# Aggregation of a graph layer with the gathered rows as the stationary side, 40 columns streaming, and a ninth row buffer

## The chip, the core and the metric

The kernel runs on one core of one Trainium2 chip. The metric is the device time of one execution in microseconds (us); lower is better. The median of three runs stands for a kernel. One more execution is recorded by the hardware profiler, and the rows in this document come from such recordings.

## The reference

There are N = 12500 nodes with D = 128 features and M = 200000 edges, sorted by destination node. All is float32. Cut to what matters:

```python
h = relu(layernorm(x))
Qv, Ku = h @ W_Q.T, h @ W_K.T
score = einsum('md,md->m', Qv[dst], Ku[src]) / sqrt(128) * exp(-edge_weight)
keep  = rank of the edge among its node's edges < 16        # the 16 best edges of a node
w     = where(keep, exp(score - max over the node's kept edges), 0)
alpha = w / (sum of w over the node)
agg   = segment_sum(alpha[:, None] * (h[src] @ W_msg.T), dst)
out   = x + relu(h @ W_self.T + agg)
```

The kernel sums the rows first and multiplies by W_msg afterwards: per node it forms the sum over edges of w times h[src], and then divides by the sum of w and multiplies by W_msg.

## The kernel before

**Prologue.** The node rows are normalised and written to a table `h_tab` in HBM. Constants are made, and the gathers of the first groups start.

**Groups and chunks.** The edges are cut into chunks of 128 edges, one edge to a partition, and 14 chunks make a group (`GC` = 14; there are `G` = 112 groups). A group's window of nodes can begin inside its last chunk and end in the first chunk of the next group, so each group works on up to 15 chunks (`NJ` = 15): chunk 14 of a group reads the first row block of the next group. Because the edges are sorted, the edges of chunk j of a group fall on 40 neighbouring nodes (`WN` = 40) that begin at 8·j − 16 in the group's window of 128 nodes.

**Gathers.** For each chunk GpSimd (POOL) issues one indirect DMA that fetches 128 rows of `h_tab`, 512 bytes each, into one block of the tile `hs` (128 partitions x 14 blocks x 128). `let_go(g, k)` does this for two chunks: VectorE (DVE) copies their indices to a small tile `ix`, and POOL issues the gathers. `hs` has 8 buffers, so the first gather of group g must wait until the last reader of group g − 8 is through. Two late blocks of some groups (`lateSP`, `lateACT`) are fetched row by row from the queues of SyncE (SP) and ScalarE (ACT) instead.

**The loop.** The order of the work is written out by hand. Step i of the loop holds stages of several groups: `q_to_edges` and `scores` for group i, `slots_by_node` and `slots_out` for i − 1, `best`, `kept_to_edges`, `on_edges`, `exps` for i − 2, `weights`, `sums` and `sums_out` for i − 3, the turning and `products` for i − 4, `output` and `store` for i − 5; `far_of`, `edges_turned`, `away` and `places` prepare the node patterns of group i + 1. Each engine works through its own list in this order. The pieces of the gathers are let go by `more(0)` to `more(6)`, spread over the step: `more(0)` after `weights`, `more(1)` just before `best`, `more(2)` just after it, `more(3)` and `more(4)` among the scores, `more(5)` after the second half of `sums`, `more(6)` at the end. In the steady loop `more(0)` to `more(4)` let go pieces 2 to 6 of group i + 4, and `more(5)` and `more(6)` pieces 0 and 1 of group i + 5.

**The banks.** The tile `et` is one PSUM bank: columns 0 to 151 take `slots_by_node`, 256 to 296 `node_by_slots`, and 384 to 511 the sums. The tile `so` is another: four blocks of 128 columns for the turned rows, the queries, the turned sums, and the products. One more bank, `a`, is passed back and forth by TensorE (PE) and ACT in `far_of`, `edges_turned` and `away`.

**The aggregation.** `weights` (L734) writes, for each chunk, the 128 x 40 pattern of edge weights into `alz`, in which a chunk has a stretch of 160 columns that is zero elsewhere. `sums` (L744) then runs one float32 matmul for each chunk: the stationary side is a slice of 128 columns of `alz`, mostly zeros, placed so that the 40 filled columns lie at the chunk's nodes; the streaming side are the 128 gathered rows' 128 features. All 15 add up to one 128 x 128 block, nodes by features. Half of them (`sums(g, 0)`, seven chunks) stand in the middle of a step, the other half (`sums(g, 1)`, eight chunks) after the third block of queries. A float32 matmul shows as two weight loads (LDWEIGHTS, engine PEld) and two matmuls (PE) in the trace. `sums_out` (L749) copies the block out of PSUM and scales each node by the reciprocal `rden`; `sums_turned` (L752) turns it on PE, `sums_turned_out` (L756) copies it out, and `products` (L759, L760) multiplies by the two weight matrices and adds.

Of the kernel before, what the change touches and what calls it, by code (L numbers as in the profile page):

```python
# [10 lines left out]
F32 = mybir.dt.float32  # L11
# [4 lines left out]
AF = mybir.ActivationFunctionType  # L16
# [9 lines left out]
P = 128  # L26
# [9 lines left out]
GC = 14  # L36
NJ = GC + 1

KM = 40

WN = 40
# [14 lines left out]
PRE = 16  # L56
STEP = 8
WW = STEP * (NJ - 1) + WN
# [3 lines left out]
def lead(j):  # L62
    return STEP * j - PRE
# [7 lines left out]
def upper(ap):  # L71

    return ap.bitcast(BF16).rearrange("p (n two) -> p n two", two=2)[:, :, 1]
# [8 lines left out]
def gnn_layer(  # L82
# [27 lines left out]
    nc = tc.nc  # L110
    N, D = x.shape
# [18 lines left out]
    const = ctx.enter_context(tc.tile_pool(name="const", bufs=1))  # L130
# [7 lines left out]
    def bank(tag, bufs):  # L138
        return psum.tile([P, 512], F32, tag=tag, bufs=bufs, name=tag)

    ident = const.tile([P, P], F32, name="ident")
    ones = const.tile([P, 1], F32, name="ones")
    onerow = const.tile([1, P], F32, name="onerow")
    zrow = const.tile([1, WW], BF16, name="zrow")


    alz = [const.tile([P, NJ * (WW + STEP)], F32, name=f"alz{i}") for i in range(2)]
    sl1 = [const.tile([P, NJ, KM + 1], F32, name=f"sl1{i}") for i in range(2)]
    slots = const.tile([P, KM], F32, name="slots")
    nvec = const.tile([P, 1], F32, name="nvec")  # L150
# [5 lines left out]
    wmsgT = const.tile([P, P], F32, name="wmsgT")  # L156
# [16 lines left out]
    rows_pool = ctx.enter_context(tc.tile_pool(name="rows", bufs=1))  # L173
# [3 lines left out]
    T = [{} for _ in range(G)]  # L177

    def gather(g, j0, j1, index, table=h_tab):
        if j0 == 0:  # L180
            T[g]["hs"] = rows_pool.tile([P, GC, D], F32, name="hs", bufs=8)
        for j in range(j0, j1):
            nc.gpsimd.indirect_dma_start(  # L183
                out=T[g]["hs"][:, j, :], out_offset=None, in_=table[0:N, :],
                in_offset=bass.IndirectOffsetOnAxis(ap=index(j), axis=0))
# [7 lines left out]
    for name, (_, _, p0, rate, j) in STREAMS.items():  # L193
        m = 0
        while rate:
            ready = p0 + (P * m + P - 1) // rate + 1
            g = max(ready, RAW)
# [62 lines left out]
    def raw_begun(g):  # L260
        normed(T[g]["hs"], 0, 1, *T[g]["raw"])
# [28 lines left out]
    with tc.tile_pool(name="edges", bufs=1) as ep, ExitStack() as stage:  # L290
# [51 lines left out]
        nc.gpsimd.iota(nvec, pattern=[[0, 1]], base=0, channel_multiplier=1,  # L342
                       allow_small_or_imprecise_dtypes=True)

        jj, eq = (alz[0][0:32, NJ * KM * k:NJ * KM * (k + 1)].rearrange("p (j k) -> p j k", k=KM) for k in range(2))
        nc.gpsimd.iota(jj, pattern=[[1, NJ], [0, KM]], base=0, channel_multiplier=0,
                       allow_small_or_imprecise_dtypes=True)
        nc.gpsimd.iota(dst_r, pattern=[[1, RL + P]], base=1 << 21, channel_multiplier=0)
# [2 lines left out]
        k = RF if REM else RF - 1  # L351
# [2 lines left out]
                              bass.AP(dst.tensor, dst.offset + p0 * RW - HALO, [[RW, p1 - p0], [1, RL + P]]))  # L354
        nc.sync.dma_start(dst_r[k:k + 1, 0:HALO + M - k * RW], dst[k * RW - HALO:M].rearrange("(p c) -> p c", p=1))
        load_rows(ew_r, ew)
        nc.gpsimd.memset(alz[1], 0.0)
        nc.vector.memset(ones, 1.0)
        nc.vector.memset(onerow, 1.0)
        nc.vector.memset(zrow, 0.0)  # L360
# [39 lines left out]

        for j in range(NJ):
            nc.vector.memset(w0[:, j:j + 1], float(lead(j)))
        nc.vector.memset(alz[0], 0.0)
        for k in range(2):
            nc.vector.memset(sl1[k][:, :, KM:], 1.0)
        for g in range(2):
# [43 lines left out]
        for j0 in range(0, NJ, 4):  # L450
            j1 = min(j0 + 4, NJ)
            pt = bank("q", 3)
            for j in range(j0, j1):
                nc.tensor.matmul(pt[:, (j - j0) * RR:(j - j0 + 1) * RR], lhsT=rel[:, j * P:(j + 1) * P],
                                 rhs=upper(ident[0:RR, 0:RR]), start=True, stop=True)
# [87 lines left out]
    with tc.tile_pool(name="win", bufs=2) as win:  # L543

        so = bank("s", 1)
        et = bank("e", 1)

        def rows_of(g, j):
            if (g, j) in slow:
                return T[g]["late", j]  # L550
            return T[g]["hs"][:, j, :] if j < GC else T[g + 1]["hs"][:, 0, :]
# [179 lines left out]
        def weights(g):  # L731
            n, kept = chunks[g], T[g]["kept"]
            nc.vector.tensor_tensor(kept[:, 0:n], T[g]["up"][:, 0:n], kept[:, 0:n], op=OP.mult)
            nc.vector.tensor_tensor(alz[g % 2].rearrange("e (j w) -> e j w", w=WW + STEP)[:, 0:n, 0:WN],  # L734
                                    T[g]["ow"][:, 0:n, :], bc(kept[:, 0:n], WN), op=OP.mult)


        def sums(g, part, at=None):
            n = chunks[g]
            if part == 0:  # L740
                T[g]["pa"] = et[:, 384:384 + P] if at is None else at
            half = n // 2
            for j in range(half) if part == 0 else range(half, n):
                nc.tensor.matmul(T[g]["pa"], lhsT=alz[g % 2][:, WW * j + PRE:WW * j + PRE + P],  # L744
                                 rhs=rows_of(g, j), start=(j == 0), stop=(j == n - 1))

        def sums_out(g):
            T[g]["agn"] = win.tile([P, D], F32, name="agn")
            nc.scalar.activation(T[g]["agn"], T[g]["pa"], AF.Copy, scale=T[g]["rden"])  # L749

        def sums_turned(g):
            nc.tensor.transpose(so[:, 2 * P:3 * P], T[g]["agn"], ident)  # L752

        def sums_turned_out(g):
            T[g]["aggT"] = win.tile([P, P], F32, name="aggT")
            nc.scalar.copy(T[g]["aggT"], so[:, 2 * P:3 * P])  # L756

        def products(g):
            nc.tensor.matmul(so[:, 3 * P:4 * P], lhsT=T[g]["hT"], rhs=wselfT, start=True, stop=False)  # L759
            nc.tensor.matmul(so[:, 3 * P:4 * P], lhsT=T[g]["aggT"], rhs=wmsgT, start=False, stop=True)  # L760

        def output(g):
            T[g]["o"] = win.tile([P, D], F32, name="o")
# [50 lines left out]
        def at(g, stage, *args):  # L814
            if 0 <= g < G:
                stage(g, *args)


        for i in range(-3, G - 1):
            at(i + 3, load_nodes)  # L820
            for k, _ in enumerate(rows_named("SP", i)):
                rows_asked("SP")
                if k == 0:
                    at(i - 1, load_x)
            if not rows_at.get(("SP", i)):
                at(i - 1, load_x)
            if i == G - 2:
                load_x(G - 2)
                load_x(G - 1)
            if i == 8:  # L830
                nc.sync.dma_start(h_tab[N:N + P, :], zpad)
                nc.sync.dma_start(x_end[XT:XT + P, :], zpad)
                nc.sync.dma_start(x_end[0:XT, :], x[N - XT:N, :])
            def raw(part):
                if i in (1, 2):
                    raw_finished(i + 1, part)

            def more(k):

                if i in (-1, 0, 1):  # L840
                    g = i + 6
                else:
                    g, k = (i + 4, k + 2) if k < 5 else (i + 5, k - 5)
                    if g < 8:
                        return
                if i >= -1 and g < G:
                    let_go(g, k)

            at(i, q_to_edges, 0)
            at(i - 5, output)  # L850
            at(i - 5, store)
            at(i - 3, weights)
            more(0)
            at(i - 4, sums_turned)
            at(i + 1, far_of, 0)
            at(i - 4, sums_turned_out)
            at(i + 1, q_out)
            at(i, q_to_edges, 1)
            at(i + 1, far_of, 1)
            rows_asked("ACT", ACT_ROWS // 8)  # L860
            raw(0)
            for b in range(3):
                at(i - 1, slots_by_node, b)
            at(i + 1, far_of, 2)
            more(1)
            at(i - 2, best)
            more(2)
            at(i - 2, sum_of_exps)
            at(i - 1, slots_out)
            raw(1)  # L870
            at(i, q_to_edges, 2)
            at(i + 1, far_of, 3)
            raw(2)
            at(i + 2, h_turned)
            at(i, scores, 0)
            more(3)
            at(i + 1, to_edges)
            rows_asked("ACT", ACT_ROWS * 5 // 16)
            at(i + 2, h_turned_out)
            at(i - 2, kept_to_edges)  # L880
            at(i - 1, node_by_slots)
            at(i + 1, edges_turned)
            at(i - 3, sums, 0)
            at(i, scores, 1)
            more(4)
            at(i + 1, away, 0)
            at(i, q_to_edges, 3)
            at(i - 2, one_over_sum)
            at(i + 1, away, 1)
            rows_asked("ACT")  # L890
            at(i - 3, sums, 1)
            at(i, scores, 2)
            at(i - 2, on_edges)
            more(5)
            at(i + 1, away, 2)
            at(i - 3, sums_out)
            at(i - 4, products)
            at(i - 2, exps)
            at(i + 1, places)
            for _ in rows_named("ACT", i + 1):  # L900
                pass
            rows_asked("ACT", ACT_ROWS * 3 // 8)
            at(i, scores, 3)
            at(i, scores_in_slots)
            if i == 0:
                raw_stats(2)
                raw_stats(3)
                raw_begun(2)
                raw_begun(3)
            if i in (1, 2):  # L910
                raw_finished(i + 1, 3)
            more(6)
            at(i + 2, q_made)
            if i > 0 and later:
                later.pop(0)()
# [3 lines left out]
        blocks = -(-chunks[L] // 4)  # L919

        def turned(g):
            sums_turned(g)
            sums_turned_out(g)

        def begun(g):
            sums(g, 0, bank("a", 1)[:, 0:P])

        def all_slots(g):
            for b in range(3):
# [78 lines left out]
    with tc.tile_pool(name="gen", bufs=1) as gen, tc.If(nc.values_load(  # L1008
# [116 lines left out]
        with tc.For_i(0, NT, 1) as T:  # L1125
# [16 lines left out]
            _, e16, rden = softmax_rest(gen, cand[:, 0:TOPK])  # L1142
# [40 lines left out]
```

## Time and profile before

| what | value |
|---|---|
| median of three runs | 3100.45 us (3090.87 to 3109.37) |
| the profiled execution, its own time | 3112.28 us |
| its span from the first to the last instruction | 3110.5 us |
| mean granted TensorE clock over the span | 0.741 of full speed |
| busy: PE, PEld, DVE, ACT, POOL | 66%, 54%, 41%, 33%, 47% of the span |
| DMA | 144.38 MB, mean 46 GB/s |

In the rows, the columns of a group are: line, engine, operation, out<-in, shapes and count, then busy time in us and the mean in ns of one, then the idle time of the engine just before them with what ended it. In a timeline they are start, duration, engine, line, operation, count, and in brackets the idle time before it with its releaser. The releaser "remote" means that the semaphore moved when no recorded instruction of this core ended. PE rows end where a model puts the end of the matmul, so neighbouring matmuls overlap in them; the distance from start to start is the throughput.

### The profile page before, as it was taken

The page shows a single profiled execution, that of the slowest core. Times are in us where ns is not written, and L with a number is a line of the kernel's source. Part 1 is how long each engine was busy: PE and PEld are TensorE (multiplying, and loading weights), DVE is VectorE, ACT ScalarE, POOL GpSimd, SP SyncE. Part 2 cuts the span into 40 slices and gives each one's busy share as a digit, 9 for nine tenths or more (in the row PEclk, how much of TensorE's full clock was granted, in tenths as well). Part 3 has the DMA queues.
Part 4 walks back from the last instruction along what each step waited for, and adds up shares of the span by engine and source line. Part 5 has one row for each costly group of instructions (what it writes and reads, how often), then busy time and mean ns, then how long its engine had stood idle before and what let it go on. Part 6 is the DMA issues. An engine that isn't in the chain of part 4 may idle for free. (4 is left out here: it accounts for less than half of the span.)

```text
span 3110.5 us, 55712 instructions
## 1 busy us (share of the span) xinstructions
PE 2052.1 (66%) x13800; PEld 1692.2 (54%) x13801; DVE 1264.1 (41%) x7016; ACT 1041.8 (33%) x2190; POOL 1457.7 (47%) x1529
## 2 busy tenths in 40 slices
PE   0256666666677667676676666776676666667667
PEld 0145555555555555555565555555565555555556
DVE  4453334433344334443433333434434433344346
ACT  4443323333333233333333333333333332333333
POOL 6524444444444444444444445444445444444440
PEclk9867777767777776777777777767767777777779
DMA  8201111111111111111111111111111111111110
GB/s 218 62 24 43 50 43 42 43 39 44 43 42 44 42 44 42 43 42 42 44 44 42 42 43 44 42 40 43 44 44 44 43 42 42 44 43 41 42 40 12
DMA packets 113004, 144.38 MB, mean 46 GB/s; under 512 B 36775, under 2 KB 86567, under 8 KB 111904
## 3 DMA queue, kind: packets, MB, share of 16 engines
q0 software_dynamic: 48512, 99.39, 12.6%
q1 hardware_dynamic: 59038, 40.04, 4.7%
q8 instruction: 109, 1.79, 0.2%
q14 instruction: 225, 1.84, 0.2%
q10 hardware_dynamic: 5120, 1.32, 0.2%
HBM read 126.79 MB, written 14.40 MB: 45 GB/s over the span
## 5 line engine op out<-in xcount | busy, mean ns | idle before, releaser
L183 POOL DMA_INDIRECT hs<-h_tab,ix x1456 | 1394.9, 958 | 1540.6 <-PE e L744 605.4
L744 PEld LDWEIGHTS e<-hs,alz 128*128 128x128 f32 x3142 | 612.1, 296 | 291.9 <-issue 280.5
L744 PE MATMUL e<-hs,alz 128*128 128x128 f32 x3142 | 668.9, 393 | 0.0
L642 PE MATMUL q<-q,to_e 128*128 128x128 f32 x3348 | 589.9, 324 | 44.9 <-issue 42.9
L642 PEld LDWEIGHTS q<-q,to_e 128*128 128x128 f32 x3348 | 545.9, 234 | 121.5 <-issue 87.5
L604 ACT ACTIVATE far<-a,minus 128x512 bf16<-128x512 f32 (+1 forms) x447 | 294.6, 659 | 891.9 <-issue 344.2
L653 DVE SCALAR_TENSOR_TENSOR prod<-hs,dec_all,q 128x128 f32<-128x128 f32 x1623 | 470.2, 342 | 133.6 <-remote 60.1
L602 PE MATMUL a<-rel,ident 112*128 112x512 bf16 (+1 forms) x447 | 211.0, 472 | 426.0 <-issue 264.4
L627 ACT ACTIVATE aw<-a 128x400 bf16<-128x400 f32 x336 | 169.4, 504 | 836.7 <-PE a L625 450.4
L683 DVE TENSOR_SCALAR ell<-slots,e 128x40 f32<-128x40 f32 x112 | 27.9, 249 | 933.6 <-remote 390.2
L625 PE MATMUL a<-minus_at,pdT 32*128 32x400 bf16 x336 | 146.6, 436 | 376.1 <-ACT aw L627 245.4
L669 PE MATMUL e<-opo,sl 128*41 128x40 f32 x3348 | 236.9, 252 | 34.0 <-issue 33.9
L669 PEld LDWEIGHTS e<-opo,sl 128*41 128x41 f32 x3348 | 215.7, 168 | 43.5 <-issue 31.3
L667 PEld LDWEIGHTS <-zrow 1*41 1x41 bf16 x112 | 11.3, 101 | 412.3 <-issue 412.2
L609 ACT ACTIVATE to_e<-far 128x1920 f32<-128x1920 bf16 x112 | 201.3, 1797 | 3.4
L764 DVE SCALAR_TENSOR_TENSOR o<-s,x_t 128x128 f32<-128x128 f32 x112 | 32.6, 291 | 403.2 <-ACT up L729 350.1
L625 PEld LDWEIGHTS <-pdT 32*128 32x128 bf16 x336 | 31.4, 94 | 190.5 <-ACT pdT L618 122.9
L631 ACT ACTIVATE opo<-aw 128x1200 f32<-128x1200 bf16 x112 | 134.7, 1202 | 0.1
L653 DVE DVE_READ_ACCUMULATOR prod<-hs,dec_all,q 128x1 f32 x1623 | 132.0, 81 | 0.0
L219 DVE COPY ix<-idx_all 128x2 int32<-128x2 int32 (+1 forms) x747 | 126.1, 183 | 0.0
L712 PEld LDWEIGHTS <-to_e 128*128 128x128 bf16 x1674 | 68.0, 111 | 94.4 <-DVE km L695 88.0
L712 PE MATMUL x<-km,to_e 128*128 128x43 bf16 x1674 | 76.7, 202 | 58.4 <-DVE km L695 58.3
(197 smaller groups left out, 1868.0 us busy)
## 6 DMA issues: line engine op xcount, KB each, us to landing
lateSP<-h_tab SPq DMA_DIRECT2D x3968, 0.5 KB
lateACT<-h_tab ACTq DMA_DIRECT2D x2560, 0.5 KB
hs<-h_tab,ix POOLq DMA_INDIRECT x1456
h_r<-h_tab SPq DMA_DIRECT2D x112, 64.0 KB
x_t<-in_x_dram SPq DMA_DIRECT2D x108, 64.0 KB
out_dram<-o SPq DMA_DIRECT2D x108, 64.0 KB
xg<-in_x_dram SPq DMA_DIRECT2D x2, 1400.0 KB
h_tab<-xg SPq DMA_DIRECT2D x2, 1400.0 KB
```

What stands on the lines that cost most here:

```text
L183: nc.gpsimd.indirect_dma_start(out=T[g]["hs"][:, j, :], out_offset=None, in_=table[0:N, :], in_offset=bass.IndirectOffsetOnAxis(ap=index(j ...
L602: nc.tensor.matmul(pr[:, 0:n1 - n0], lhsT=upper(ident[0:RR, g:g + 1]).to_broadcast([RR, P]), rhs=rel[:, n0:n1], start=True, stop=True)
L604: nc.scalar.activation(T[g]["far"][:, n0:n1], pr[:, 0:n1 - n0], AF.Square, bias=minus)
L609: nc.scalar.activation(T[g]["to_e"][:, 0:n], T[g]["far"][:, 0:n], AF.Relu, bias=1.0, scale=-1.0)
L625: nc.tensor.matmul(pr[:, 0:400], lhsT=T[g]["pdT"], rhs=minus_at.rearrange("k w j s -> k (w j s)")[:, n0:n1], start=True, stop=True)
L627: nc.scalar.activation(T[g]["aw"][:, n0:n1], pr[:, 0:400], AF.Square)
L631: nc.scalar.activation(T[g]["opo"].rearrange("e w j s -> e (w j s)"), T[g]["aw"], AF.Relu, bias=1.0, scale=-1.0)
L642: nc.tensor.matmul(pq[:, (j - j0) * P:(j - j0 + 1) * P], lhsT=T[g]["to_e"][:, j * P:(j + 1) * P], rhs=T[g]["q"], start=True, stop=True)
L653: nc.vector.scalar_tensor_tensor(prod, rows_of(g, j), dec_all[:, c:c + 1], T[g]["pq", b][:, (j % 4) * P:(j % 4 + 1) * P], op0=OP.mult, op1 ...
L669: nc.tensor.matmul(et[0:KM + 1, STEP * j:STEP * j + WN], lhsT=sl1[g % 2][:, j, :], rhs=T[g]["ow"][:, j, :], start=False, stop=(j == n - 1))
L712: nc.tensor.matmul(px[:, j, 0:KM + 3], lhsT=upper(T[g]["to_e"][:, j * P:(j + 1) * P]), rhs=upper(T[g]["km"]), start=True, stop=True)
L744: nc.tensor.matmul(T[g]["pa"], lhsT=alz[g % 2][:, WW * j + PRE:WW * j + PRE + P], rhs=rows_of(g, j), start=(j == 0), stop=(j == n - 1))
```

## The change

- The aggregation is turned round. The stationary side is now a chunk's gathered rows (128 edges x 128 features), the streaming side the chunk's 40 columns of weights, and the result has features on the partitions and nodes along the columns. Each chunk adds to its own 40 columns of a stretch of 152, so one more matmul with a row of zeros first opens the whole stretch.
- `alz` shrinks from 15 x 160 to 15 x 40 columns; its two memsets go, and the helper tiles that lay in it in the prologue get tiles of their own.
- The result is already turned. `sums_out` becomes a plain copy; `messages` multiplies it by W_msg (a float32 matmul where the transpose was); `messages_out` scales by `rden` while it copies out; `products` adds that with an identity matmul.
- `hs` has nine buffers, and in the loop every piece of the gathers belongs to one group later than before: pieces 2 to 6 of group i + 5 and pieces 0 and 1 of group i + 6. Step 2 lets go a whole group (8).

```diff
-    alz = [const.tile([P, NJ * (WW + STEP)], F32, name=f"alz{i}") for i in range(2)]
+    alz = [const.tile([P, NJ, WN], F32, name=f"alz{i}") for i in range(2)]
...
-            T[g]["hs"] = rows_pool.tile([P, GC, D], F32, name="hs", bufs=8)
+            T[g]["hs"] = rows_pool.tile([P, GC, D], F32, name="hs", bufs=9)
...
-        jj, eq = (alz[0][0:32, NJ * KM * k:NJ * KM * (k + 1)].rearrange("p (j k) -> p j k", k=KM) for k in range(2))
+        jj, eq = (ep.tile([32, NJ, KM], F32, name=f"jk{k}") for k in range(2))
...
-        nc.gpsimd.memset(alz[1], 0.0)
...
-        nc.vector.memset(alz[0], 0.0)
...
-            nc.vector.tensor_tensor(alz[g % 2].rearrange("e (j w) -> e j w", w=WW + STEP)[:, 0:n, 0:WN],
+            nc.vector.tensor_tensor(alz[g % 2][:, 0:n, :],
                                     T[g]["ow"][:, 0:n, :], bc(kept[:, 0:n], WN), op=OP.mult)
...
             if part == 0:
-                T[g]["pa"] = et[:, 384:384 + P] if at is None else at
+                T[g]["pa"] = et[:, 304:304 + WW] if at is None else at
+                nc.tensor.matmul(T[g]["pa"], lhsT=zrow[:, 0:P], rhs=zrow, start=True, stop=False)
             half = n // 2
             for j in range(half) if part == 0 else range(half, n):
-                nc.tensor.matmul(T[g]["pa"], lhsT=alz[g % 2][:, WW * j + PRE:WW * j + PRE + P],
-                                 rhs=rows_of(g, j), start=(j == 0), stop=(j == n - 1))
+                nc.tensor.matmul(T[g]["pa"][:, STEP * j:STEP * j + WN], lhsT=rows_of(g, j),
+                                 rhs=alz[g % 2][:, j, :], start=False, stop=(j == n - 1))
 
         def sums_out(g):
+            T[g]["aggT"] = win.tile([P, P], F32, name="aggT")
+            nc.scalar.copy(T[g]["aggT"], T[g]["pa"][:, PRE:PRE + P])
+
+        def messages(g):
+            nc.tensor.matmul(so[:, 2 * P:3 * P], lhsT=T[g]["aggT"], rhs=wmsgT, start=True, stop=True)
+
+        def messages_out(g):
             T[g]["agn"] = win.tile([P, D], F32, name="agn")
-            nc.scalar.activation(T[g]["agn"], T[g]["pa"], AF.Copy, scale=T[g]["rden"])
-
-        def sums_turned(g):
-            nc.tensor.transpose(so[:, 2 * P:3 * P], T[g]["agn"], ident)
-
-        def sums_turned_out(g):
-            T[g]["aggT"] = win.tile([P, P], F32, name="aggT")
-            nc.scalar.copy(T[g]["aggT"], so[:, 2 * P:3 * P])
+            nc.scalar.activation(T[g]["agn"], so[:, 2 * P:3 * P], AF.Copy, scale=T[g]["rden"])
 
         def products(g):
             nc.tensor.matmul(so[:, 3 * P:4 * P], lhsT=T[g]["hT"], rhs=wselfT, start=True, stop=False)
-            nc.tensor.matmul(so[:, 3 * P:4 * P], lhsT=T[g]["aggT"], rhs=wmsgT, start=False, stop=True)
+            nc.tensor.matmul(so[:, 3 * P:4 * P], lhsT=ident, rhs=T[g]["agn"], start=False, stop=True)
...
             def more(k):
-                if i in (-1, 0, 1):
+                if i in (-1, 0, 1, 2):
                     g = i + 6
                 else:
-                    g, k = (i + 4, k + 2) if k < 5 else (i + 5, k - 5)
-                    if g < 8:
+                    g, k = (i + 5, k + 2) if k < 5 else (i + 6, k - 5)
+                    if g < 9:
                         return
...
-            at(i - 4, sums_turned)
+            at(i - 4, messages)
...
-            at(i - 4, sums_turned_out)
+            at(i - 4, messages_out)
```

The calls after the loop, for the last groups, change in the same way.

More of the change, by code (lines that the diff above doesn't have):

```diff
@@ L921, in turned @@
         def turned(g):
-            sums_turned(g)
-            sums_turned_out(g)
+            messages(g)
+            messages_out(g)
         def begun(g):
-            sums(g, 0, bank("a", 1)[:, 0:P])
+            sums(g, 0, bank("a", 1)[:, 0:WW])
         def all_slots(g):
```

## Prediction

> **What bounds the kernel now.** I read the page first: no engine is full.
>
> ```profile
> span 3110.5 us, 55712 instructions
> ...
> PE 2052.1 (66%) x13800; PEld 1692.2 (54%) x13801; DVE 1264.1 (41%) x7016; ACT 1041.8 (33%) x2190; POOL 1457.7 (47%) x1529
> ```
>
> POOL, which issues the gathers, idles for half of the span, so I asked its waits next (total us, times, longest).
>
> ```profile
> POOL hs L183 <- PE e L744: 605.4, 99, 7.9
> POOL hs L183 <- DVE prod L653: 462.0, 106, 6.2
> ```
>
> There are about 106 laps of one group each, and in nearly each the first gather waits for `sums`. The timeline shows the lap: eight gathers, a pause, six gathers, a pause.
>
> ```profile
> 1504.56 0.95 POOL L183 DMA_INDIRECT hs<-h_tab,ix  x1 [7.72 <-PE e L744]
> ...
> 1513.60 0.94 POOL L183 DMA_INDIRECT hs<-h_tab,ix  x1 [0.30 <-issue]
> 1518.66 0.94 POOL L183 DMA_INDIRECT hs<-h_tab,ix  x1 [4.11 <-DVE prod L653]
> ...
> 1524.90 0.94 POOL L183 DMA_INDIRECT hs<-h_tab,ix  x1 [0.30 <-issue]
> 1531.98 0.95 POOL L183 DMA_INDIRECT hs<-h_tab,ix  x1 [6.13 <-PE e L744]
> ```
>
> What happens in the pauses, from the timeline of all engines, is one chain:
>
> ```profile
> 1511.83 0.38 PE L602 MATMUL a<-rel,ident 112*128 112x512 bf16 x1 [3.53 <-ACT far L604]
> 1512.30 2.32 PE L669 MATMUL e<-opo,sl 128*41 128x40 f32 x30
> 1516.26 0.25 DVE L683 TENSOR_SCALAR ell<-slots,e 128x40 f32<-128x40 f32 x1 [8.64 <-PE a L602]
> 1518.23 0.16 DVE L219 COPY ix<-idx_all 128x2 int32<-128x2 int32 x1
> 1524.34 0.17 DVE L719 TENSOR_TENSOR up<-up,s 128x15 f32<-128x15 f32 x1 [2.08 <-remote]
> 1527.38 0.50 ACT L627 ACTIVATE aw<-a 128x400 bf16<-128x400 f32 x1 [5.68 <-remote]
> 1528.36 3.78 PE L744 MATMUL e<-hs,alz 128*128 128x128 f32 x16
> ```
>
> One lap is 1531.98 − 1504.56 = 27.42 us: 9.04 to the eighth gather; 2.66 until `ell` starts, although the PE work that it reads (L669) ended at 1514.62, 1.64 before; 2.40 until the next gather; 6.24 to the sixth; 2.48 until ACT's `aw`; 0.98 until the second half of `sums`; 3.62 from there to the next lap's first gather. In the two pauses nothing runs that would account for the first 1.6 us, and the waits there are put down to "remote" or to work long done. Such waits belong to the gathers: L719 follows L718 on the same engine, 2.08 us late here, 0.03 us late in a stretch without gathers.
>
> ```profile
> 228.37 0.20 DVE L718 TENSOR_REDUCE up<-x 128x15 f32<-128x45 f32 x1
> 228.60 0.17 DVE L719 TENSOR_TENSOR up<-up,s 128x15 f32<-128x15 f32 x1
> ```
>
> So I read: while gathers are in flight, hand-overs between instructions are late, and what waits is let go some 1.6 us after the last gather of a batch. PE, ACT and DVE work that ends before that costs nothing. Of all that the change touches, only the 3.62 us of the second half of `sums` lie on the path.
>
> **The change part by part.**
>
> *Sums, second half (16 load-and-matmul pairs).* How long is a pair whose load is 128 columns and whose stream is 40? No such pair is in the trace. The parts are, at the same low clock: the first load of a run alone, with 128 and with 41 columns, and a matmul within a run, with 128 and with 40.
>
> ```profile
> L744 PEld LDWEIGHTS e<-hs,alz 128*128 128x128 f32 x1 | 0.3, 287 | 4.6 <-issue 4.6
> L669 PEld LDWEIGHTS e<-opo,sl 128*41 128x41 f32 x1 | 0.1, 145 | 0.1
> L744 PE MATMUL e<-hs,alz 128*128 128x128 f32 x11 | 2.6, 421 | 0.0
> L669 PE MATMUL e<-opo,sl 128*41 128x40 f32 x26 | 2.0, 269 | 0.0
> ```
>
> Loads: (287 − 145)/(128 − 41) = 1.63 ns a column, so 128 columns are 209 ns. Streams: (421 − 269)/88 = 1.73 ns a row, and eleven L744 matmuls take 2.6 us, of which the pace is (2.6 − 0.42)/10, about 0.21 us (0.2135 from the starts of the 16: (3.78 − 0.16 − 0.42)/15). So a load of 128 costs what a stream of 128 costs, and the two overlap: in turn they would be 0.42. With a 40-row stream the load remains, and the pace stays at 0.2135. I take that: turning the sum round trades a stream for nothing, since the load was the same length all along. Bounds for the pace: 0.0707 from L669, (2.32 − 0.27)/29, if only the stream counted; 0.209 + 0.067 = 0.276 if a short stream could no longer cover the next load. What remains is the shorter last stream: 0.421 − 0.269 = −0.15 us a lap.
>
> *The clock.* The mean over all matmuls of L744 in the loop, and over the last groups:
>
> ```profile
> L744 PE MATMUL e<-hs,alz 128*128 128x128 f32 x3142 | 668.9, 393 | 0.0
> L744 PE MATMUL a<-hs,alz 128*128 128x128 f32 x104 | 13.1, 279 | 0.2 <-DVE alz L734 0.2
> 3080.44 3.59 PE L744 MATMUL a<-hs,alz 128*128 128x128 f32 x30
> ```
>
> One takes 421 ns at the low clock and 279 at the high one, where 30 have a pace of (3.59 − 0.28)/29 = 0.114. The mean 393 says that (393 − 279)/(421 − 279) = 0.80 run at the low clock. The granted clock around a second half, and in the batch behind it:
>
> ```profile
> 1500.93:1504.64 3.71, 3.71 (x17) 3.48 (x17) 1.42 (x8) 0.50 (x1) 0.09 (x1) 0.50 0.01 2
> 1505.40:1508.20 2.80, 2.80 (x24) 2.69 (x24) 1.30 (x5) 1.75 (x4) 2.19 (x3) 0.99 0.27 73
> ```
>
> (Columns: busy us and count of PE, PEld, DVE, ACT, POOL; granted clock; DMA share; GB/s.) 3.7 us of solid matmuls at 0.50 are followed by 0.99. If what counts is the stream, it is solid no longer after the change (about 67 of 213 ns), the clock is not raised, and the 20% at the high clock go too: 14 x 0.20 x (0.2135 − 0.114) = +0.28 us a lap. [...]
>
> Together: (−0.15 + 0.28) x 106 = +13 us. If the clock is raised as before, it is −0.15 x 106 = −16; if it falls, the 22 or so 128x128 matmuls of L759 to L642 behind (2.80 us) lose 22 x 0.0995 = 2.2 us, hidden beneath the eight gathers: PE has 3.53 us of idle before L602 at 1511.83 and `ell` waits 1.64 us beyond L669. I cost that at nothing.
>
> *Sums, first half, and the zero matmul* lie under the six gathers; the zero matmul is like L667's. *The turned copy, `messages`, `products`*: a float32 matmul in two passes for the one-pass transpose, one pair for another in `products`, the same two ACT copies in the other order: about one pair (0.3 us) more, under the eight gathers.
>
> ```profile
> L667 PE MATMUL e<-zrow 1*41 1x152 bf16 x112 | 31.2, 278 | 0.0
> L752 PE MATMUL s<-ident,agn 128*128 128x128 f32 x112 | 30.7, 274 | 3.0 <-DVE rden L705 1.9 <-DVE o L764 1.0
> ```
>
> Cover gone, they would cost 0.28 + 0.27 us a lap, +58; I take 0 in the loop and +1 for the last groups, where nothing is gathered.
>
> *Ninth buffer, one group more ahead.* With eight buffers, the first gather of i + 5 overwrites group i − 3; with nine, that of i + 6 also overwrites i − 3. The same wait stands at the same place, on the same half of `sums`, with the same POOL queue behind it. Rows arrive a lap earlier, and no wait for gathered rows is among POOL's or PE's large ones. At the start one step (2) gains a batch; at the end one more step runs without gathers:
>
> ```profile
> 207.00:225.00 18.00, 11.95 (x71) 9.43 (x71) 9.99 (x50) 9.16 (x20) 0.00 (x0) 0.63 0.05 13
> 3049.00:3067.00 18.00, 16.80 (x164) 14.33 (x163) 10.80 (x58) 10.65 (x23) 0.00 (x0) 0.91 0.03 9
> ```
>
> A step without gathers takes about 18 us, one with them 27, so +9 and −9: 0, bounds −9 and +9.
>
> *The last groups* have no cover and the high clock: at the low one, 104 matmuls x 0.0995 = +10; I take +8.
>
> *Prologue.* Two memsets go, on POOL and DVE, worth −4.3 if both were on the path and 0 if neither; I take −2.
>
> ```profile
> L357 POOL MEMSET alz<- 128x2400 f32 x1 | 2.3, 2282 | 0.0
> L403 DVE MEMSET alz<- 128x2400 f32 x1 | 2.1, 2058 | 0.5 <-issue 0.5
> ```
>
> **Sum:** +13 + 1 + 0 + 8 − 2 = +20 on the profiled execution's own 3112.3, so 3132. It stands 0.4% over the median of the runs; times 3100.45/3112.28 = 0.9962 that is **3120 us**.
>
> **The rivals.**
>
> 1. *The clock is raised as before* (loads count as work): −16 − 1 = −17, 3095, as a median 3083. For it: PEld is as busy as PE in the solid stretch. Against: L669's stretch, loads and streams of equal length, tells nothing apart.
>
> 2. *Load and stream go in turn, each at half the pace I gave it.* The trace allows that reading: 213.5/256 = 0.83 ns a column, load and stream added up, and L669's 70.7/81 = 0.87. Then 128 + 40 columns cost 140 ns. The pace now is 0.80 x 0.2135 + 0.20 x 0.114 = 0.194 in the mean, so 14 x (0.140 − 0.194) − 0.15 = −0.90 a lap, −96; with the last groups (104 x 0.026 = +3) and −1, −94: 3018, as a median 3007. Against: the first load's own length, 287 against 145. [...]
>
> 3. *The load is cheap and overlaps*: half of the slope, 0.1045 us: 14 x (0.1045 − 0.194) − 0.15 = −1.40 a lap, −148, with −2 for the rest 2962, as a median 2951.
>
> 4. *Slower by more: the clock's fall is not covered.* The 2.2 us lost behind the second half pass through to `ell`. Place: PE before L669; it decides as soon as the cover is under 2.2. With the 1.64 of `ell` as cover it is 0.55 x 106 = 58 more, 3190, as a median 3178. For it: the same clock rules the whole batch. Against: 3.53 us of idle on PE before it.
>
> That the change doesn't do what it says can be for the ninth buffer only, and is in the sum as such.
>
> **How the numbers follow.** My forecast (pace kept by the load, clock low) has 0.42; rival 1 0.15; rival 2 0.22, since one slope of modelled ends speaks against it; rival 3 0.08; rival 4 0.13. Measurement can tell about 0.5%, 15.5 us. The forecast is +20 of unknowns of about ±15: slower 0.27, same 0.15. Rival 1, at −17, is split, faster 0.07 and same 0.08. Rivals 2 and 3 are faster, 4 slower. So faster 0.37, same 0.23, slower 0.40. The range from 3005 to 3180 takes in all but rival 3 and what lies beyond rivals 2 and 4. The forecast's own range is 3100 to 3140.
>
> **What would show it right or wrong.** Right: the second half of `sums` as 16 matmuls at 0.21 us from start to start, their durations 0.27, granted clock 0.50 in them and in the eight gathers' first microseconds; 99 or so waits of POOL for L743's matmuls of about 6 us; laps of 27.4. A pace of 0.14 or less is rival 2 or 3; 0.99 after the second half is rival 1; `ell` right behind L669's end is rival 4. The forecast is wrong altogether if POOL's first gather no longer waits for `sums`, or if the batches of gathers change in length.

## The result and the profile after

The changed kernel takes 3176.8 us against 3098.7 us, a ratio of 1.0255 (95% interval 1.022 to 1.0289): +78 us. In the two profiled executions the spans differ by 65.1 us. The page of the changed kernel, its header, busy times and the clock in 40 slices:

```profile
span 3175.6 us, 56157 instructions
...
PE 2284.1 (72%) x14024; PEld 1916.6 (60%) x14025; DVE 1268.7 (40%) x7015; ACT 1045.3 (33%) x2190; POOL 1450.2 (46%) x1528
...
PEclk9966666656666666666656666666666566666666
```

Only PE and PEld are clearly busier; the granted clock has fallen from 0.741 to 0.657 in the mean. The queries of the kernel before, then the queries and the sums of the changed one (count, busy us, mean ns):

```profile
L642 PE MATMUL q<-q,to_e 128*128 128x128 f32 x3348 | 589.9, 324 | 44.9 <-issue 42.9
```

```profile
L640 PE MATMUL q<-q,to_e 128*128 128x128 f32 x3348 | 732.3, 388 | 25.1 <-issue 24.4
...
L743 PE MATMUL e<-alz,hs 128*128 128x40 f32 x3142 | 666.5, 391 | 0.0
L743 PE MATMUL a<-alz,hs 128*128 128x40 f32 x104 | 20.6, 377 | 0.0
```

Turning the sums did next to nothing to their own busy time in the loop (668.9 us before). In the last groups (tile `a`) they take 377 ns apiece instead of 279, and the queries, which the change does not touch, went from 324 to 388. The wait of POOL for the sums stands where it stood (99 times, 605.4 us before):

```profile
POOL hs L183 <- PE e L743: 673.3, 102, 15.4
POOL hs L183 <- DVE prod L651: 466.6, 107, 6.0
```

A second half of the sums, from the timeline:

```profile
1522.03 0.49 PE L623 MATMUL a<-minus_at,pdT 32*128 32x400 bf16 x1 [4.26 <-ACT aw L625]
1522.45 3.64 PE L743 MATMUL e<-alz,hs 128*128 128x40 f32 x16
1525.93 0.94 POOL L183 DMA_INDIRECT hs<-h_tab,ix  x1 [6.09 <-PE e L743]
```

From its start to POOL's next gather it is 3.48 us where the lap quoted in the prediction had 3.62. In the 63 halves of the changed kernel that show as one run of 16, the pace after the first pair is 0.2133 us from start to start, and from the start of the half to the gather it is 3.54 us in the mean, as it was before. So that stretch neither gained nor lost. Where the 65.1 us went, by three marks that both traces have (the pattern L661, now L659, of the sixth group and of the ninth from the end):

| stretch | before | after | difference |
|---|---|---|---|
| start to the sixth group's pattern | 283.7 | 291.9 | +8.2 |
| 98 steps of the loop | 2638.4 | 2677.1 | +38.7 |
| from there to the end | 188.4 | 206.6 | +18.2 |

And one lap, in its parts, as a mean over the laps of each trace:

| part of the lap | before | after |
|---|---|---|
| first to last of the eight gathers | 8.90 | 8.81 |
| to the first of the six | 5.32 | 5.37 |
| first to last of the six | 5.65 | 5.66 |
| to the second half of the sums | 3.71 | 4.12 |
| to the next lap's first gather | 3.33 | 3.37 |
| lap | 26.91 | 27.33 |

The loss sits in the part ahead of the second half, and there it has two values: about 3.5 us in some laps, about 5.1 in others. Before, 20 of 110 laps are over 4.5 us, after the change 44. A lap of the long kind, from the changed kernel's timeline:

```profile
1481.73 0.69 ACT L602 ACTIVATE far<-a,minus 128x512 bf16<-128x512 f32 x1 [4.02 <-remote]
...
1482.84 1.91 PE L640 MATMUL q<-q,to_e 128*128 128x128 f32 x8
...
1484.40 0.95 POOL L183 DMA_INDIRECT hs<-h_tab,ix  x1 [4.46 <-DVE prod L651]
1484.55 0.52 PE L600 MATMUL a<-rel,ident 112*128 112x384 bf16 x1
1485.11 0.58 ACT L602 ACTIVATE far<-a,minus 128x384 bf16<-128x384 f32 x1 [0.90 <-PE a L600]
1485.72 1.80 ACT L607 ACTIVATE to_e<-far 128x1920 f32<-128x1920 bf16 x1
...
1490.67 0.95 POOL L183 DMA_INDIRECT hs<-h_tab,ix  x1 [0.30 <-issue]
1492.98 0.26 ACT L616 CAST pdT<-a 32x128 bf16<-32x128 f32 x1 [4.82 <-remote]
1493.30 0.51 PE L623 MATMUL a<-minus_at,pdT 32*128 32x400 bf16 x1 [3.58 <-ACT pdT L616]
1493.74 1.65 PE L640 MATMUL q<-q,to_e 128*128 128x128 f32 x6
1495.32 0.51 PE L623 MATMUL a<-minus_at,pdT 32*128 32x400 bf16 x1
1495.76 2.35 PE L743 MATMUL e<-alz,hs 128*128 128x40 f32 x10
```

and the same step in the short lap that the prediction walked through, from the timeline of the kernel before:

```profile
1512.24 0.69 ACT L604 ACTIVATE far<-a,minus 128x512 bf16<-128x512 f32 x1
...
1518.97 1.80 ACT L609 ACTIVATE to_e<-far 128x1920 f32<-128x1920 bf16 x1
...
1521.45 0.26 ACT L618 CAST pdT<-a 32x128 bf16<-32x128 f32 x1
...
1522.83 0.94 PE L642 MATMUL q<-q,to_e 128*128 128x128 f32 x6
```

In the short lap the second `far` goes through while gathers still start (the last at 1513.60); `to_e` ends 2.11 us after the first of the six gathers (1518.66), `pdT` is cast at once, and `away` and six queries are done beneath the batch. In the long lap that `far` is held until after the eight gathers (4.02 us, "remote"), all behind it comes later, `to_e` ends 3.12 us after the first of the six, and now the hand-over to `pdT` is held as well, 4.82 us, until 2.3 us after the last gather. `away`, six queries at a granted clock of 0.50 (1.65 us, where the short lap's six take 0.94 at 1.00) and `away` again then stand between the batch and the sums. Over the laps, `to_e` ends mostly either about 2.1 or about 3.1 us after that gather: up to 2.2 us the cast was early in 79 of 79 laps before and 54 of 54 after, over 2.8 us it was late in 22 of 22 and 38 of 39. Between the two lie 2 laps before and 9 after.

At the end of the program the clock is lower too (columns as in the prediction), first of the kernel before, then of the changed one:

```profile
3080.00:3095.00 15.00, 11.30 (x124) 10.35 (x125) 13.20 (x65) 2.54 (x11) 0.30 (x1) 1.00 0.02 7
3095.00:3110.50 15.50, 7.19 (x65) 6.47 (x64) 2.98 (x10) 1.48 (x5) 3.68 (x4) 0.86 0.06 17
```

```profile
3125.00:3150.00 25.00, 22.31 (x175) 20.22 (x174) 15.97 (x78) 4.10 (x15) 0.00 (x0) 0.64 0.02 7
3150.00:3175.60 25.60, 16.90 (x77) 15.09 (x77) 3.40 (x13) 1.85 (x6) 3.98 (x4) 0.50 0.04 10
```

### The profile page after: what moved, and what is told of

The parts are those of the page before. It is cut to its first block, busy times and chain, and to the rows that moved or that the text cites. A ratio compares the mean times of both kernels' runs of the same rounds, so it can differ in the third digit from the quotient of the medians.

```text
span 3175.6 us, 56157 instructions
## 1 busy us (share of the span) xinstructions
PE 2284.1 (72%) x14024; PEld 1916.6 (60%) x14025; DVE 1268.7 (40%) x7015; ACT 1045.3 (33%) x2190; POOL 1450.2 (46%) x1528
## 5 line engine op out<-in xcount | busy, mean ns | idle before, releaser
L640 PEld LDWEIGHTS q<-q,to_e 128*128 128x128 f32 x3348 | 689.5, 295 | 152.8 <-issue 111.0
L640 PE MATMUL q<-q,to_e 128*128 128x128 f32 x3348 | 732.3, 388 | 25.1 <-issue 24.4
L743 PEld LDWEIGHTS e<-alz,hs 128*128 128x128 f32 x3142 | 632.3, 304 | 186.4 <-issue 171.6
L743 PE MATMUL e<-alz,hs 128*128 128x40 f32 x3142 | 666.5, 391 | 0.0
L623 PE MATMUL a<-minus_at,pdT 32*128 32x400 bf16 x336 | 167.1, 497 | 342.9 <-ACT pdT L616 166.6
L600 PE MATMUL a<-rel,ident 112*128 112x512 bf16 (+1 forms) x447 | 213.2, 477 | 247.7 <-ACT far L602 148.6
L667 PE MATMUL e<-opo,sl 128*41 128x40 f32 x3348 | 192.6, 213 | 135.2 <-issue 133.8
L667 PEld LDWEIGHTS e<-opo,sl 128*41 128x41 f32 x3348 | 160.7, 125 | 132.4 <-issue 122.5
L710 PEld LDWEIGHTS <-to_e 128*128 128x128 bf16 x1674 | 74.4, 115 | 54.7 <-DVE km L693 46.0
L616 ACT CAST pdT<-a 32x128 bf16<-32x128 f32 x112 | 28.5, 254 | 237.4 <-remote 232.9
```

Of the source, the lines that this page charges most:

```text
L600: nc.tensor.matmul(pr[:, 0:n1 - n0], lhsT=upper(ident[0:RR, g:g + 1]).to_broadcast([RR, P]), rhs=rel[:, n0:n1], start=True, stop=True)
L623: nc.tensor.matmul(pr[:, 0:400], lhsT=T[g]["pdT"], rhs=minus_at.rearrange("k w j s -> k (w j s)")[:, n0:n1], start=True, stop=True)
L640: nc.tensor.matmul(pq[:, (j - j0) * P:(j - j0 + 1) * P], lhsT=T[g]["to_e"][:, j * P:(j + 1) * P], rhs=T[g]["q"], start=True, stop=True)
L667: nc.tensor.matmul(et[0:KM + 1, STEP * j:STEP * j + WN], lhsT=sl1[g % 2][:, j, :], rhs=T[g]["ow"][:, j, :], start=False, stop=(j == n - 1))
L743: nc.tensor.matmul(T[g]["pa"][:, STEP * j:STEP * j + WN], lhsT=rows_of(g, j), rhs=alz[g % 2][:, j, :], start=False, stop=(j == n - 1))
```

## The experiments

The theory after the result: less streaming lowers the clock; the lower clock costs time in the loop where `pdT` comes late, and at the end. The rivals: the lead (the gathers let go one group earlier) and the ninth buffer, or PE's longer work as such. The runs went to three chips, e1 to e4, e5 to e8 and e9 to e12, and the kernel before takes 2190, 3146 and 2188 us on them. So every ratio is to the kernel before on the same chip, and the first question became what differs between the chips.

### e5, the kernel before, and e6, the changed kernel, on one chip

> The kernel before, unchanged, for its trace on the chip of these runs. On the chip of the runs e1 to e4 it took 2190 us where it took 3099 us in the comparison that was forecast. Theory: that difference is the hand-overs that the gathers hold back, so on a chip like that one L719 follows L718 without the 0.4 to 2 us of the profile shown, and the pauses between the batches of gathers are 2 to 3 us instead of 5 to 7; on a chip like the first one the trace repeats itself, 3099 us. Rival (the chip's clock or its gathers differ): the gathers are not 1.25 us apart, or the granted clock is another by more than 0.05.

> The changed kernel, unchanged. On a chip like the first one 3177 us, 2.5% over the kernel before. On a chip where hand-overs are quick PE work is not hidden beneath late hand-overs, so the lower clock shows in full: 2300 to 2340 us, as with the turned sums alone (2329), if ninth buffer and lead are neutral; 2230 or less if the lead brings something of its own there. Clock about 0.66 and 0.75 in the two cases.

This chip is like that of the forecast: 3149.8 us for e5, clock 0.740; e6 3239.7 us, ratio 1.0295 (1.0277 to 1.0314), clock 0.652. The lap is 27.26 and 27.96 us, `pdT` late in 46 and in 79 of 108 laps; the part ahead of the second half went from 4.01 to 4.64 us in the mean, 0.63 of the 0.70. No trace of the unchanged kernel before was taken on a quick chip. The nearest is e10 (the kernel before with one step moved, 2170.1 us of span; first POOL's timeline, then DVE's):

```profile
1009.46 0.94 POOL L183 DMA_INDIRECT hs<-h_tab,ix  x1 [0.30 <-DVE rden L706]
1010.71 0.94 POOL L183 DMA_INDIRECT hs<-h_tab,ix  x1 [0.30 <-issue]
...
1013.25 0.94 POOL L183 DMA_INDIRECT hs<-h_tab,ix  x1 [0.35 <-PE e L744]
```

```profile
1010.23 0.20 DVE L718 TENSOR_REDUCE up<-x 128x15 f32<-128x45 f32 x1
1010.46 0.17 DVE L719 TENSOR_TENSOR up<-up,s 128x15 f32<-128x15 f32 x1
```

The gathers are 1.25 us apart as on the other chips, but L719 follows L718 after 0.03 us in the middle of a batch, and the next batch starts (1013.25) at the spacing of the gathers, without a pause. In all 112 laps of e10 that gap is at most 0.04 us; in e5 it is over 0.1 us in 60 of 112, up to 3.1 us. So what the expectation of e5 says of quick chips is seen in e10, not in e5 itself. Its rival is met in part as well: the granted clock there is another, 0.883 against 0.740. But the clock can't be the 900 us: the turned sums of e11, below, take 2331.5 us on a quick chip at 0.751. And from the last gather to the end, where none is in flight, e10 takes 93.6 us and e5 93.0. The difference lies where gathers are in flight, and I read it as late hand-overs.

### e7 and e2, the stream made solid again

```diff
-                nc.tensor.matmul(T[g]["pa"][:, STEP * j:STEP * j + WN], lhsT=rows_of(g, j),
-                                 rhs=alz[g % 2][:, j, :], start=False, ...)
+                c0 = min(WN * j, NJ * WN - P)
+                nc.tensor.matmul(T[g]["pa"][:, 0:P], lhsT=rows_of(g, j),
+                                 rhs=alz[g % 2].rearrange("e j w -> e (j w)")[:, c0:c0 + P], ...)
```

> The changed kernel with 128 streamed columns in each matmul of the sums, as in the run e2 (the sums are not the reference's), now beside the changed kernel itself. Clock theory: faster than the changed kernel although it streams three times as much: on a chip like the first one 3105 to 3120 us, clock 0.74; on a quick one 2184 us, clock 0.88, against 2300 to 2340. Rival: as slow as the changed kernel, within 0.5%.

> The changed kernel, but each matmul of the sums streams 128 columns of the weights instead of its own 40, into the same 128 columns of the bank (the sums are then not the reference's); rows stay the stationary side, loads and order as in the changed kernel. Clock theory: pace unchanged at 0.213 us, because the load sets it, but the stream is solid again, so the granted clock goes back to about 0.74, late casts of pdT from 51 to 25 or so of 108 laps (26 x 1.65 = -43 us), the last groups back to the higher clock (-20 to -26): 3105 to 3120 us. Rival (the loss is in the roles of the operands, the additional matmuls or the lead, and the clock is a by-stander): 3165 us or more, since more is streamed and nothing else is changed.

e7: 3157.8 us, ratio 1.0047 (1.003 to 1.0064), 82 us faster than the changed kernel beside it, with three times the columns streamed. The clock is 0.731, the lap 27.20 us, `pdT` late in 51 of 108. e2: 2184.3 us, ratio 0.9962 (0.994 to 0.9983), clock 0.879. By the three marks of the first table, e5, e6 and e7 take 284.6, 297.4 and 289.7 us at the start, 2673.9, 2738.8 and 2672.5 in the 98 steps, and 189.5, 211.8 and 189.3 at the end. ACT's wait ahead of `pdT` (total us, times, longest), in e5, e6 and e7:

```profile
ACT pdT L618 <- remote: 199.9, 73, 5.1
```

```profile
ACT pdT L616 <- remote: 342.8, 93, 5.4
```

```profile
ACT pdT L616 <- remote: 196.6, 71, 5.2
```

So 82 of the 94 us that e6 loses come back with the stream, and the clock with them, from 0.652 to 0.731 where e5 has 0.740: in this kernel the clock falls because the sums stream less, and nearly the whole loss hangs on that. All the rest of the change together (operand roles, additional matmuls, copies, buffer, lead) is worth 0.3 to 0.6% on this chip; in the traces of e5 and e7 it is about 5 us at the start and nothing in the loop or at the end.

### e8, the load cut to 40 columns

```diff
+                f = D if j == n - 1 else WN
-                nc.tensor.matmul(T[g]["pa"][:, ...], lhsT=rows_of(g, j), ...)
+                nc.tensor.matmul(T[g]["pa"][0:f, ...], lhsT=rows_of(g, j)[:, 0:f], ...)
```

> The changed kernel, but all matmuls of the sums except a group's last load only 40 of the 128 features as the stationary side (the sums of the other features are left out). It measures the load. If the load sets the pace, start to start falls from 0.213 to about 0.07 us, as in L667 (41 columns, 40 rows), and the second half from 3.4 to about 1.3 us; the time falls by up to 2 us a lap on a chip like the first one (3177 - 210 = 2970 us), and to 2190 or less on a quick one. Rival (load and stream in turn, or the stream with its own fixed cost): a pace of 0.14 us or more.

3073.2 us, ratio 0.9778 (0.976 to 0.9796). One second half and the gather behind it:

```profile
1509.25 1.74 PE L744 MATMUL e<-alz,hs 128*40 128x40 f32 x16
1510.67 0.95 POOL L183 DMA_INDIRECT hs<-h_tab,ix  x1 [5.50 <-PE e L744]
```

1.42 us instead of 3.48: 14 of the 16 pairs are shorter by 2.06/14 = 0.147, so a pace of about 0.066. Here the load sets the pace: 0.213 us with 128 columns loaded, 0.066 with 40. The stream adds nothing to it, so the two overlap: in the second halves that run wholly at a granted clock of 0.50, the pace is 0.2133 us before the change, with 128 columns streamed (46 halves), and 0.2133 after it, with 40 (108 halves). Against e6 the time falls by 166 us, not by the 210 expected: the lap falls by 1.46 us only, from 27.96 to 26.50, although this half is 1.96 shorter in the mean, since `pdT` is now late in 100 of 108 laps (ACT waits 409.3 us for it in all). So the clock is not all that makes the cast late. The clock is 0.663, hardly above the 0.652 of e6, with the loads of the sums cut to a third: they did not hold it up.

### e1 and e11, the turned sums alone

```diff
-            T[g]["hs"] = rows_pool.tile([P, GC, D], F32, name="hs", bufs=9)
+            T[g]["hs"] = rows_pool.tile([P, GC, D], F32, name="hs", bufs=8)
...
-                if i in (-1, 0, 1, 2):
+                if i in (-1, 0, 1):
...
-                    g, k = (i + 5, k + 2) if k < 5 else (i + 6, k - 5)
-                    if g < 9:
+                    g, k = (i + 4, k + 2) if k < 5 else (i + 5, k - 5)
+                    if g < 8:
```

> The turned aggregation alone: eight buffers and the old lead, all else as in the changed kernel. Clock theory: the whole loss comes from the turned sums (less streaming, so a lower clock), and buffer and lead are neutral: 3177 us within 10, mean granted clock about 0.66, the second half of the sums at a pace of 0.213 us, and in about 45 of 108 laps the cast of pdT only after the last gather of the six. Rival (the longer lead and the additional step without gathers cost the time): back to about 3121 us, what the sums alone were forecast to cost, or less.

> As in e1, eight buffers and the old lead with the turned sums, to be had on a chip with late hand-overs. Theory: buffer and lead are neutral there (one wait for the same half of the sums in every lap; one lap's gathers more at the start, a step without gathers more at the end), so 1.025 to 1.03 of the kernel before, as the whole change. Rival (the lead has a price or a gain of its own): outside 1.02 to 1.035. On a chip with quick hand-overs 1.064 again.

Both fell on chips with quick hand-overs (ahead of the two steps L716 and L717 DVE idles 3.8 us in all, where e5 has 261.2 ahead of the same two, L718 and L719): 2329.5 us, ratio 1.0643 (1.061 to 1.0676), and 2331.5 us, 1.0649 (1.0611 to 1.0687), clock 0.754 and 0.751. So what e1 was to decide on the chip of the forecast stays undecided. Here the turned sums alone cost over 6%; I put that to PE time that no longer hides beneath held hand-overs, which no run takes apart. The sums of e10, which leaves them as they were, and of e11:

```profile
L744 PE MATMUL e<-hs,alz 128*128 128x128 f32 x3142 | 415.2, 282 | 0.0
```

```profile
L743 PE MATMUL e<-alz,hs 128*128 128x40 f32 x3142 | 571.3, 353 | 0.0
```

The old sums run close to the full clock there (282 ns, where the prediction's rows have 279 at the full clock and 421 at the low one), the turned ones lose it (353 ns; granted clock 0.883 in the mean of e10, 0.751 in e11). The whole change was not run on such a chip, and these two not on one with late hand-overs, so what the lead does by itself has no run of its own.

### e12, nine buffers with the old lead

The diff is that of e1 without its first pair of lines.

> The changed kernel with nine buffers but the old lead, so that the first gather of a lap overwrites a group whose sums ended a lap before: the buffer is used for slack, not for distance. Theory: POOL no longer waits for L743 in every lap; the eight gathers start when the indices are copied, some 2.5 us earlier, and the lap falls by 2 to 2.5 us: -200 to -260 us on a chip with late hand-overs, 0.95 to 0.97 of the kernel before. Rival (the gathers that start earlier hold the last hand-overs of the lap back, and what is gained at the start is lost at the next one): 1.01 or more.

2327.0 us, ratio 1.0643 (1.0603 to 1.0682): nothing against e11 on the same chip. POOL's waits in e11, then in e12:

```profile
POOL hs L183 <- PE e L743: 197.3, 98, 9.6
POOL hs L183 <- DVE prod L651: 163.5, 121, 3.3
```

```profile
POOL hs L183 <- DVE prod L651: 265.8, 126, 4.9
...
POOL hs L183 <- DVE ix L219: 80.8, 81, 2.0
POOL hs L183 <- PE e L743: 35.0, 90, 1.7
```

The buffer did remove the wait for the sums (197 to 35 us), and the gathers wait as long for DVE instead; the laps are 19.75 and 19.74 us. Whether it brings something on a chip with late hand-overs stays open.

### e3, e4, e9, e10: steps moved so that pdT comes earlier

e3 (changed kernel) and e4 (kernel before) put the last `far_of` ahead of the third block of queries; e9 and e10 put `edges_turned` ahead of `to_edges`.

```diff
+            at(i + 1, far_of, 3)
             at(i, q_to_edges, 2)
-            at(i + 1, far_of, 3)
```

> The changed kernel with one step of the written order moved: the last far_of (L600, 384 columns) goes ahead of the third block of queries (eight 128x128 matmuls) instead of behind it. Theory: at the low clock these eight matmuls (1.7 us) delay far, then to_e, then the cast of pdT by 1 us, so that it falls into the time in which the gathers hold hand-overs back, and the lap becomes 1.65 us longer; with far ahead, to_e ends 2.1 us after the first of the six gathers in nearly all laps, the 51 late casts go to under 10 and the time falls by 45 x 1.65 = 70 us to about 3105 us, at the same clock of 0.66. Rival (late casts are a symptom, the lap is longer because PE itself has too much work at the low clock): 3165 us or more.

> The kernel before with the same step moved. Theory: it has 29 late casts of pdT in 108 laps too; nearly all go, so 25 x 1.65 = -41 us, about 3058 us. Rival (the late casts do not set the lap): 3099 us within 10.

```diff
+            at(i + 1, edges_turned)
             at(i + 1, to_edges)
...
-            at(i + 1, edges_turned)
             at(i - 3, sums, 0)
```

> The changed kernel with edges_turned (L613 and the cast of pdT) moved ahead of to_edges in the written order, so that the cast no longer stands behind to_e (1.8 us) on ACT. Theory: what the lower clock costs in the loop is the late cast (79 of 108 laps on the last chip, 1.65 us each). With the cast early in nearly all laps, the second half of the sums starts 3.5 us after the last gather of the batch in all of them: -79 x 1.65 = -130 us, so from 1.03 to about 0.99 of the kernel before, at an unchanged clock of 0.65. Rival (PE is simply slower, the late cast a symptom): 1.02 to 1.03. On a chip with quick hand-overs no gain is expected: about as the changed kernel.

> The kernel before with the same step moved. Theory: its own late casts (29 to 46 of 108 laps) go too: -50 to -75 us, 0.975 to 0.985 of the kernel before, clock 0.74. Rival: 1.00 within 0.5%. On a chip with quick hand-overs 1.00 within 1%.

All four fell on chips with quick hand-overs (3.8 us of idle in all ahead of the same two DVE steps), where ACT does not wait for a held `pdT` in the first place (e3 and e4 have no wait there, e9 and e10 33.4 us each, on PE, at most 0.4 us at a time), so they do not decide what they were made for. e3: 2232.6 us, 1.0215 (1.0169 to 1.0261); that is 97 us below e1, the turned sums alone on the same chip, and no run tells whether the moved step or the lead did it. e4: 2391.8 us, 1.0921 (1.0889 to 1.0952). PE now waits ahead of the queries, 222 times where e10, on the other quick chip, has 112 waits of 368.8 us in all, and the clock is 0.765. That wait alone does not make up the loss:

```profile
PE a L602 <- ACT far L604: 456.6, 222, 5.0
```

e9: 2357.4 us, 1.0772 (1.0725 to 1.082), some 1% above e11, the turned sums without the lead. e10: 2176.4 us, 0.9946 (0.9925 to 0.9967), on this chip a little faster than the kernel before, and the fastest there of those that do the whole computation.

## Why the prediction was right, and where it was not

The sign and the range held (3005 to 3180 for 3176.8), but only just, and with luck. The forecast's +20 us became +78, and its own range, 3100 to 3140, was missed. Slower had a chance of 0.40 against 0.37 for faster. And the range reaches to 3180 on account of rival 4, whose place for the loss was not the one found.

- *The pace of a pair.* Right: 0.2135 forecast, 0.2133 measured, and e8, at 0.066 with loads of 40 columns, shows that the load sets it. Rivals 2 and 3, 0.30 together, are out with their 0.140 and 0.1045 us.
- *The clock falls.* Right: rival 1 is out. Over the nine microseconds of the eight gathers, the mean of the laps went from 0.87 to 0.71. In the lap of 1495 the second half runs at 0.50, and the batch behind it begins at 0.50, where the prediction's row had 0.99:

```profile
1495.76:1499.32 3.56, 3.56 (x17) 3.48 (x16) 1.42 (x8) 0.50 (x1) 0.93 (x1) 0.50 0.01 1
1500.00:1503.00 3.00, 3.00 (x15) 3.00 (x16) 1.31 (x5) 1.74 (x4) 2.39 (x3) 0.50 0.29 79
```

- *The sums in the lap.* +0.13 us forecast; from the second half's start to the gather it is +0.04 in the mean. A small miss, but a term in it was wrong: the matmuls take 414 ns (median), not the 0.27 us that were to come of the shorter stream, and the gather follows the start of the last one by 0.26 us, as by 0.27 before. What the half shown above gains, 0.14 us, lies between its first two starts, 0.23 us apart instead of 0.37.
- *The fall is hidden beneath the eight gathers, and costs nothing.* This is the step that failed, +0.4 us a lap on the first chip and +0.6 on the second. The 3.53 and 1.64 us that I took for slack were measured in a lap of the short kind. I had seen hand-overs held while gathers run (L719 by 2.08 us), and used it only to hide work; the other side is that work that misses its moment is held until the batch ends, as `pdT` in the long lap for 4.82 us. The second `far` was held past the eight gathers in 26 of 99 laps before and in 85 after (46, 96 and 47 in e5, e6 and e7), and `pdT` was late nearly only in such laps. Rival 4 had the price, 3178, and the trigger, but another place: `ell` is as late as it was (5.32 to 5.37 us to the six gathers), the time passes through `pdT`. Being held is not enough, though: of the laps after the change in which the second `far` was held, only about half had a late cast.
- *Start and end.* At the start +9 for the additional batch and −2 for the prologue were forecast, and +8.2 came. That they are so close is luck: on the second chip e6 has +12.8, of which +5.1 are left in e7. At the end the sum was −9 + 8 + 1 = 0 where +18.2 were measured. I let only the 104 last matmuls lose the full clock, but all work of the last 50 us runs at 0.50 to 0.64 instead of 0.86 to 1.00 (the clock's part is 22.5 us between e7 and e6); and the −9 for the step without gathers did not come: e7's end is as long as e5's (189.3 and 189.5).
- *Buffer and lead.* The wait for L743 stands at the same place, 102 times 6.6 us, as forecast. No run separates their price; together with all else but the stream they come to the 0.3 to 0.6% of e7.

What stays open: why the slower PE makes the second `far` miss its moment. L600 starts at nearly the same distance from the first gather (6.8 to 7.3 us, medians) in laps of both kinds, and no run with late hand-overs moved that step. Nor does the clock tell the laps of one trace apart: over the eight gathers it is 0.71 in the mean in laps of both kinds after the change, and 0.87 in both before. That the late `pdT` costs some 1.6 us is read from six traces of four kernels, not shown by a run that takes it away. Shown is that here the clock follows the stream (0.652 in e6, 0.731 in e7), and that the time comes back with it; the way between, through `far` and `pdT`, is read from the laps.

## What to carry to other kernels

Turning this matmul round emptied the stream and left the pace of a pair at 0.2133 us, since the load set it (0.066 with loads of 40 columns): compare what one load costs with what one stream costs, in rows of the trace, before counting columns. The clock was part of the price: the edit, which emptied the stream without shortening the stretch, took the granted clock from 0.741 to 0.657 and slowed the work behind it, the queries from 324 to 388 ns. And slack measured in a lap whose hand-overs came in time is not slack in a lap where one was held: here 3.53 and 1.64 us stood in one lap of the short kind, and the second `far` was held in 26 of 99 laps before the change and in 85 after it. Count the laps of both kinds.

## What the runs showed of the hardware

- The kernel before takes 2190 us on the chip of e1 to e4 and 2188 on that of e9 to e12, 3146 on that of e5 to e8, and 3099 in the comparison of the forecast. Within a batch the gathers start 1.25 us apart in e10, on a quick chip, as in the trace of the kernel before. From the last gather to the end, with none in flight, e10 and e5 take 93.6 and 93.0 us; while gathers are in flight L719 follows L718 within 0.04 us in e10, and up to 3.1 us later in e5.
- In these runs streaming held the clock up and loading did not: on one chip 0.731 with 128 columns streamed (e7), 0.652 with 40 (e6), 0.663 with 40 and loads of 40 (e8).
- At the granted clock 0.50 a float32 pair with a load of 128 columns takes 0.2133 us from start to start, with 128 columns streamed (the kernel before) and with 40 (the changed kernel); in e8, with loads of 40 columns, it is about 0.066.
